# A four-layer Mamba, attention and 13x13 convolution chain on one core: the local gate stays in its PSUM bank, two residual sums move to VectorE, and the last image's and the convolutions' edges are cut finer

## The chip, the cores and the metric

The kernel runs on one core of a Trainium2 chip, as one launch, all in fp32. The metric is the time of one execution on the device in microseconds (us), the median of the executions shown. The engines are TensorE (PE in the profile; its weight load is PEld), VectorE (DVE), ScalarE (ACT) and GpSimd (POOL); SyncE (SP) only issues transfers. SP, ACT and POOL each have a queue of transfers, and the profile shows 16 DMA engines behind them.

## The reference

`x` is (8, 384, 32, 32): B=8 images, C=384 channels, L=1024 pixels. Four layers follow each other:

```
# layer 0, per image, channels last
xn   = rmsnorm(x) * norm_w
u, z = split(xn @ in_proj.T);  u = silu(conv1d(u));  dt, Bm, Cm = split(u @ x_proj.T)
delta = softplus(dt @ dt_proj.T + b)
h[t] = exp(delta*A) * h[t-1] + delta*u*Bm ;  y[t] = sum_n h[t,n]*Cm[n]      # 16 states n
fwd  = ((y + u*D) * silu(z)) @ out_proj.T ;  bwd = the same on the reversed pixels
x1   = x + 0.5 * (0.25*(fwd + bwd) + sigmoid(dwconv3x3(xn) + b) * xn)
# layer 1
h  = conv1x1(bn(x1)); h = dwconv3x3(h); h = conv1x1(bn(h)); x1 = h + x1
q, k, v = conv1x1(x1); out = linear attention with phi(t) = exp(0.5*(2t - t*t)), 8 heads
x2 = x1 + proj(out);  x2 = x2 + mlp(layernorm(x2))                 # 384 -> 1536, gelu, -> 384
# layer 2: a sum of seven depthwise convolutions with bn: one 13x13 kernel per channel
y2 = sum_i bn_i(dwconv_i(x2))
# layer 3
xp = bn(conv1x1(y2)) + y2
out = gelu(bn(dwconv13x13(xp)) + bn(xp*w))
```

The steps that the change touches are the local gate `sigmoid(...)*xn`, the two residual sums `h + x1` and `x1 + proj(out)`, and the ways from one layer to the next after the last image.

## The kernel before

An image has two halves h of 512 pixels and three chunks c (or m) of 128 channels. A product of 128 x 128 weights with 512 columns is issued as four column quarters of 32 (`quarters`, L571, matmul at L575); `dense` (L581) makes three such products, one for each chunk of the input, into one PSUM bank. PSUM has banks under four tags: `mm` (two, `psum`) for short results, `mo` (three, `long_psum`) for results that live longer, `acc` for the scan's sums, and `du`.

**front(b)** (L676) prepares image b: rmsnorm, `project` (in-projection), `branch` (L717, the local gate) and `inner` (conv1d, dt, B and C, written to DRAM for the scan). The gate convolves a half and chunk into a short bank (`conv3`, matmuls at L595 and L600), ScalarE writes tanh from the bank into an SBUF tile `lg` (L725), and two VectorE operations (L728, L731) form `(tanh + 1) * xn` and add it to `xr`, the input read again; a transfer on GpSimd's queue writes the result. These last three are deferred by a step (`defer(1, local)`).

**scan(b)** (L814) goes over 12 units (direction d, half h, chunk c) of four rounds r with two steps i each. A step makes two `da` (exp, ScalarE, L902), `du` (VectorE, L907, into PSUM), two scan instructions `hs` (VectorE, L919), a multiplication by C on GpSimd (L928) and, after both steps, four selector matmuls into `acc` (`sums`, L600). On the way back, the gate `zr` is multiplied in (L875) and `g_d` written (L876, GpSimd's queue).

**layer1(b)** (L1002) reads x1 and g (L1009, L1010), takes the out-projection `op` (L1015, sum on VectorE L1017), the first 1x1 convolution (`h`, L1035), writes it as a padded image to `h_d`, reads that as shifted rows for the 3x3 convolution (`dw`, L638, L1042), then the second 1x1 convolution `c` (L1048), keys and values, `q`, the projection `pj` (L1147), layernorm and the MLP (`mf`, `mo`, L1228 to L1261). The residuals of `c` and `pj` are added by TensorE: an identity product `quarters(ps, ident, o, True, False)` ahead of the three products, and ScalarE evacuates with the bias (L1052, L1151). `last` (L1217) adds the MLP's and writes `x2i_d` on GpSimd's queue; `turn` (L1200) rearranges it into `x2_d`.

**Order of the work.** The driver runs the scans of the eight images in a row (48 rounds each) and, between their rounds, steps of front(b+1) and layer1(b-1) by cost and due time. At `i == rounds - 8` it takes the first step of layer1(b), its loads. A planner at the end of the file (`Plan`, `draft`, the table `BIAS` of rank shifts by engine and kind of instruction) then fixes the order on every engine; names in the profile follow the tiles.

**The tail.** After the last scan come layer1(7), with the loads of the first 20 windows `tp_a` of convolution a's weights on GpSimd's queue between its steps (`windows`), then convolution a (13x13, `conv`, L282 to L384: 96 groups of 32 matmuls over image rows `xt_a`, L364; `put2` writes `y2_d` in fours), the 1x1 convolution `pw` (16 steps t of 3 x 3 products, L410; `yp` read at L419, `xp_d` written at L424) and convolution b. There a GpSimd-queue transfer reads the rows `xt_b` (L323), two VectorE copies shift them (L337), `put3` takes gelu on ScalarE (L432) and writes `out` from GpSimd's queue (L433). Stage edges go through DRAM.

Of the kernel before, what the change touches and what calls it, by code (L numbers as in the profile page):

```python
# [17 lines left out]
P = 128  # L18
C = 384
# [54 lines left out]
def tile_layers(  # L74
# [164 lines left out]
    def load_windows(g_d, tag, n, queues):  # L239

        if not wins:
            wins["pool"] = ctx.enter_context(tc.tile_pool(name="win", bufs=1, side="right"))
        tp = wins["pool"].tile([P, NCH, TP], FP, tag="tp", name=f"tp_{tag}_{n}", bufs=N_WIN)
        for e in range(NSH):
            at = H * ((n % 2 * 2 + e) % NSH)
            win = bass.AP(
                g_d.tensor, g_d[NCH * n, e, 0, 0].offset,
                [[KT, H], [NSH * TG * KT, NCH], [1, TP]],
            )
            queues[e % len(queues)].dma_start(tp[at : at + H], win)  # L250
        wins[tag, n] = tp
# [14 lines left out]
    with tc.tile_pool(name="cx", bufs=2, reuse_waits="tile") as cxp, tc.tile_pool(  # L266
# [15 lines left out]
        def conv(g_d, src_d, last_d, tag, put, far):  # L282
# [13 lines left out]
            def load(n):  # L296
# [10 lines left out]
                if last_d is not None:  # L307
# [12 lines left out]
                src = bass.AP(  # L320
                    src_d.tensor, src_d[NCH * n, 0, 0].offset, [[RL, H], [H * RL, NCH], [1, RL]],
                )
                nc.gpsimd.dma_start(xt[at[0] : at[0] + H], src)  # L323
                xts[n] = xt

            def shift(n):
                at, xt = places(n), xts[n]
                if last_d is not None:
# [45 lines left out]
        def put2(g, ps):  # L374
# [6 lines left out]
            if g % GB == GB - 1:  # L381
                nc.gpsimd.dma_start(y2v[g - GB + 1 : g + 1].rearrange("g p n -> p g n"), hold["t"])
# [20 lines left out]
        for t in range(H // 2):  # L403
            yt = cwp.tile([P, NC, NB], FP, tag="yp", name=f"yp_{t}", bufs=3)
            nc.sync.dma_start(yt, yf[:, :, t * NB : (t + 1) * NB])
            xo = xos[t % 3]
            for m in range(NC):
                ps = cps.tile([P, HALF], FP, tag="cv", name=f"pw_{t}_{m}")
                for k in range(NC):
                    nc.tensor.matmul(  # L410
                        ps[:, 0:NB], pwt[:, k, m * P : (m + 1) * P], yt[:, k, :],
                        start=(k == 0), stop=(k == NC - 1),
                    )
                tm = cwp.tile([P, NB], FP, tag="tm", name=f"tm_{t}_{m}", bufs=3)
                nc.scalar.activation(
                    tm, ps[:, 0:NB], AF.Identity, bias=pbias[:, m, :], scale=bns("pw", m)
                )
                for r in range(2):
                    mid = xo[:, m, r, PADW : PADW + B * (W + PADW)].rearrange("p (b w) -> p b w", w=W + PADW)[:, :, 0:W]  # L419
                    nc.vector.tensor_add(  # L420
                        mid, tm[:, r * BW : (r + 1) * BW].rearrange("p (b w) -> p b w", w=W),
                        yt[:, m, r * BW : (r + 1) * BW].rearrange("p (b w) -> p b w", w=W),
                    )
            nc.gpsimd.dma_start(xf[:, :, 2 * t : 2 * t + 2, :], xo)  # L424
            if t < N_WIN:
                load_windows(g3_d, "b", t, [nc.scalar, nc.sync])
# [3 lines left out]
        def put3(g, ps):  # L430
            ot = cxp.tile([P, BW], FP, tag="ot", name=f"ot_{g}", bufs=6)
            nc.scalar.activation(ot, ps, AF.Gelu, bias=gbias[:, g : g + 1])  # L432
            nc.gpsimd.dma_start(  # L433
# [8 lines left out]
def _layers01(tc, nc, B, xv, x2_d, x2i_d, dram, ident, mean_w, eps5, eps6, one, half, minus1, vec, bns, bnt,  # L442
# [12 lines left out]
    with ExitStack() as ctx:  # L455
# [124 lines left out]
        def dense(ps, w, m, rhs, begin=True):  # L580
            for k in range(NC):  # L581
                product = quarters(
                    ps, w[:, k, m * P : (m + 1) * P], rhs[k] if isinstance(rhs, list) else rhs[:, k, :],
                    begin and k == 0, k == NC - 1,
# [93 lines left out]
        def front(b):  # L678
# [38 lines left out]
            def branch():  # L717
                t3 = tapw(taps3, f"t3_{b}")
                for h in range(2):
                    for c in range(NC):  # L720
# [3 lines left out]
                        lc = t2(f"lg_{b}_{c}_{h}")  # L724
# [9 lines left out]
                        defer(1, local)  # L734
# [77 lines left out]
        newest = []  # L812

        def scan(b):  # L814
# [36 lines left out]
            def sums(k, r, hs, made, acc, y0, zt):  # L851
# [22 lines left out]
                else:  # L874
                    nc.vector.tensor_mul(zt, acc, zt)  # L875
                    nc.gpsimd.dma_start(gv[b][:, c, cols], zt)  # L876
# [125 lines left out]
        def layer1(b):  # L1002


            xx = [None, None]
            w = wtile(outproj_t, f"wo_{b}")
            for h in (1, 0):
                xh, gh = a6(f"xx_{b}_{h}"), a6(f"g_{b}_{h}")
                nc.sync.dma_start(xh, x1v[b][:, :, bass.ts(h, HALF)])  # L1009
                nc.sync.dma_start(gh, gv[b][:, :, bass.ts(h, HALF)])  # L1010
                xx[h] = xh
                yield 0
                for m in range(NC):
                    ps = long_psum(f"op_{b}_{m}_{h}")
                    dense(ps, w, m, gh)  # L1015
                    o = xh[:, m, :]
                    nc.vector.scalar_tensor_tensor(o, ps, rsm, o, ALU.mult, ALU.add)  # L1017
                    yield 3
            w = wtile(c1_d, f"c1_{b}")

            hhs = [image6(f"hh_{b}_{h}") for h in range(2)]
            t3 = tapw(taps3b, f"t3b_{b}")
            dws = [a6(f"dw_{b}_{h}") for h in range(2)]
# [5 lines left out]

            ahead = None  # L1030
            for m, h in ((0, 1), (1, 1), (0, 0), (1, 0), (2, 1), (2, 0)):
                if (m, h) == (2, 0):
                    ahead = ready()
                ps = long_psum(f"h_{b}_{m}_{h}")
                dense(ps, w, m, xx[h])  # L1035
                nc.scalar.activation(hhs[h][1][m], rows(ps), AF.Identity, bias=bias1[:, m, :])
                put_image(h_d, b % 2, h, hhs[h][0], nc.scalar, slice(m, m + 1))
                yield 3
# [7 lines left out]
            for h in range(2):  # L1046
                for m in range(NC):
                    ps = long_psum(f"c2_{b}_{m}_{h}")  # L1048
                    o = xx[h][:, m, :]
                    quarters(ps, ident, o, True, False)  # L1050
                    dense(ps, w, m, dws[h], False)
                    nc.scalar.activation(o, ps, AF.Identity, bias=biasc[:, m, :])  # L1052
# [92 lines left out]
            for h in range(2):  # L1145
                for m in range(NC):
                    ps = long_psum(f"pj_{b}_{h}_{m}")  # L1147
                    o = xx[h][:, m, :]
                    quarters(ps, ident, o, True, False)
                    dense(ps, kvp, m, qps[h], False)  # L1150
                    nc.scalar.activation(o, ps, AF.Identity, bias=vec("proj_b", m))  # L1151
# [46 lines left out]
            behind_gelu = []  # L1198
# [18 lines left out]
            def last(h, acc):  # L1217
                for m in range(NC):
# [4 lines left out]
                    nc.gpsimd.dma_start(x2v[b][:, m, bass.ts(h, HALF)], o)  # L1223
# [4 lines left out]
            for h in range(2):  # L1228
                acc = [long_psum(f"mo_{b}_{h}_{m}") for m in range(NC)]
                for i in range(FF // C):  # L1230
                    wa = wtile(w1_d[:, i * C : (i + 1) * C], f"w1_{b}_{h}_{i}")
                    wb = wtile(w2[i * C : (i + 1) * C, :], f"w2_{b}_{h}_{i}")
                    for fs in [(0, 1), (2,)]:
# [12 lines left out]

                        def second(h=h, i=i, fs=fs, acc=acc, wb=wb, hms=hms):
# [12 lines left out]
            behind_gelu.pop()()  # L1260
# [21 lines left out]
        for b in range(B):  # L1282
            for i, _ in enumerate(scan(b)):
# [4 lines left out]
                if i == rounds - 8:  # L1288
# [483 lines left out]
def draft(nc, tc, bias):  # L1772
# [15 lines left out]
BIAS = {('Activation', 'acc<y0'): -12600,  # L1788
 ('Activation', 'bc_d<xd'): -51300,
 ('Activation', 'center<center'): -83700,  # L1790
 ('Activation', 'da<dlt'): -200,
 ('Activation', 'dl<dt'): -12400,
 ('Activation', 'dw<dw'): -147300,
 ('Activation', 'fold<fold'): -200,
 ('Activation', 'gbias<biasq_d'): -8800,
 ('Activation', 'h_d<hh'): -8500,
 ('Activation', 'hh<h'): -43100,
 ('Activation', 'hm<mf'): -98200,
 ('Activation', 'kp<phi_k'): 21100,
 ('Activation', 'kv<kvs'): 107600,  # L1800
 ('Activation', 'kvp<kvp'): 156300,
 ('Activation', 'lg<lc'): 39500,
 ('Activation', 'ms_r<ms_r'): 1000,
 ('Activation', 'ms_r<ms_s'): -114400,
 ('Activation', 'phi_k<kv_kp'): 98300,
 ('Activation', 'phi_q<q'): -245400,
 ('Activation', 'rz<den'): 1000,
 ('Activation', 'sq<xi'): -34300,
 ('Activation', 'tm<pw'): -16000,
 ('Activation', 'tp_a<g2_d'): -113400,  # L1810
 ('Activation', 'tp_b<g3_d'): 96300,
 ('Activation', 'u_d<uz'): 29000,
 ('Activation', 'uc<c1'): -700,
 ('Activation', 'uz<in'): -7500,
 ('Activation', 'var_r<var_r'): 1500,
 ('Activation', 'var_r<var_s'): -6000,
 ('Activation', 'vs<xx'): -200,
 ('Activation', 'vt<kv_vt'): 2000,
 ('Activation', 'vt<ones'): 5000,
 ('Activation', 'x2_d<turn'): 72600,  # L1820
 ('Activation', 'xd<xd'): -15500,
 ('Activation', 'xx<c2'): 1700,
 ('Activation', 'xx<pj'): -6000,
 ('Activation', 'yf_d<yt'): 5200,
 ('Activation', 'yt<acc'): -96200,
 ('Activation', 'yt<cv_a'): 32000,
 ('Activation', 'z_d<uz'): 28000,
 ('DVE', 'bias1<fold'): -199800,
 ('DVE', 'bias2<bias2'): 108300,
 ('DVE', 'bias2<bn_t'): -1200,  # L1830
 ('DVE', 'bias3<bn_t'): -28500,
 ('DVE', 'biasc<fold'): 59500,
 ('DVE', 'biasf<fold'): -175000,
 ('DVE', 'carry<hs'): 6400,
 ('DVE', 'dlt<pk'): -14500,
 ('DVE', 'du<vr'): -301300,
 ('DVE', 'dwh<pk'): 31000,
 ('DVE', 'g2<kw'): -17200,
 ('DVE', 'g3<k3'): -159500,
 ('DVE', 'hs<da'): 99000,  # L1840
 ('DVE', 'ks<m8'): -28000,
 ('DVE', 'kv<kvs'): 62700,
 ('DVE', 'lg<lg'): -11200,
 ('DVE', 'ln<xx'): -85600,
 ('DVE', 'pbias<pb'): 52300,
 ('DVE', 'pbias<pbias'): 1000,
 ('DVE', 'qp<qp'): -7200,
 ('DVE', 'uc<dl'): -23400,
 ('DVE', 'ud<uc'): -33200,
 ('DVE', 'v2<pk'): 33500,  # L1850
 ('DVE', 'var_r<var_r'): -67300,
 ('DVE', 'var_r<var_s'): -9600,
 ('DVE', 'xn<xi'): 48500,
 ('DVE', 'xo0<tm'): 16000,
# [214 lines left out]
```

## Time and profile before

| | us |
|---|---|
| median of three executions | 4565.47 (4554.04 to 4566.64) |
| the profiled execution | 4564.33 |
| its span / outside the span | 4562.5 / 1.8 |
| busy PE / DVE / POOL / ACT | 4009.3 / 3657.0 / 2771.6 / 2647.7 |
| last scan instruction ends, about | 3614 |
| layer1 of the last image | 3614 to 3972 |
| convolution a | 3982.0 to 4207.9 |
| pw | 4218.1 to 4344 |
| convolution b, last matmul | 4358.3 to 4551.3 |
| mean granted TensorE clock | 0.924 |

The span holds eight scans of about 439 us each (104.9 to 3614, in which an image's 96 steps of du and two scan instructions are about 370 us of VectorE), and the tail of 948 us. A mean busy share says little here: in the scans several engines work side by side, in the tail the stages follow each other. The bracket at the end of a timeline row is the time for which the engine was idle before it and what released it.

### The profile page before, as it was taken

What the parts mean: (1) busy time and instruction counts of PE and PEld (TensorE: products, weight loads), DVE (VectorE), ACT (ScalarE), POOL (GpSimd) and SP (SyncE); (2) the same over time, 40 slices, a digit from 0 to 9 for tenths busy, and PEclk for the clock granted to TensorE, in tenths of its full rate; (3) what the DMA queues carried; (4) which work ended last, traced back from release to release, by engine and by line L of the source; (5) the groups of instructions that cost most, each with busy time, mean ns of one, the idle gap of its engine ahead of it and who ended that gap; (6) DMA issues with size and microseconds to landing.
All of it is one profiled execution on the core that took longest, in us unless ns stands there. A gap on an engine that the chain in (4) does not pass through costs nothing.

```text
span 4562.5 us, 97044 instructions
## 1 busy us (share of the span) xinstructions
PE 4009.3 (88%) x39222; PEld 1573.9 (34%) x39222; DVE 3657.0 (80%) x3749; ACT 2647.7 (58%) x3777; POOL 2771.6 (61%) x1672
## 2 busy tenths in 40 slices
PE   5577699899999999998999999989899789987988
PEld 1122223233433332343223323432232233276467
DVE  2999989999999889998998899899999600175266
ACT  3555657875797578667866786678567413100212
POOL 2677766676667657765776577657676820143079
PEclk8578799999999999999999999999999889998999
DMA  9568776588668866885688668866844761299798
GB/s 259 174 210 273 242 239 209 188 256 264 228 207 254 251 212 204 262 258 198 215 255 249 202 226 261 237 212 215 256 144 162 186 146 48 84 223 229 224 212 183
DMA packets 651130, 975.75 MB, mean 214 GB/s; under 512 B 158280, under 2 KB 333368, under 8 KB 649144
## 3 DMA queue, kind: packets, MB, share of 16 engines
q1 hardware_dynamic: 502064, 676.48, 50.3%
q0 software_dynamic: 53392, 188.07, 13.4%
q10 hardware_dynamic: 95224, 104.98, 7.7%
q8 instruction: 309, 5.06, 0.5%
q14 instruction: 141, 1.16, 0.1%
HBM read 736.63 MB, written 232.67 MB: 212 GB/s over the span
## 4 chain that ended last, share of the span: by engine, by line
PE 42%; issue 15%; DVE 14%; DMA 11%; ACT 6%; POOL 3%; SPq 1%; ACTq 0%; POOLq 0%; DVEq 0%
DVE hs L919 9%; PE mo L575 6%; PE mf L575 6%; DVE du L907 3%; PE pj L575 3%; PE acc L595 3%; PE cv_a L364 2%; PE in L575 2%; PE kv_vt L575 2%; PE c L575 2%; ACT da L902 2%; PE kv_kp L575 2%; DMA tp_a<-g_d 2%; PE q L575 2%; DMA out<-ot 2%
## 5 line engine op out<-in xcount | busy, mean ns | idle before, releaser
L928 POOL TENSOR_TENSOR hs<-hs,bct 128x1024 f32<-128x1024 f32 x768 | 2171.8, 2828 | 845.0 <-DVE carry L924 490.0
L902 ACT ACTIVATE da<-dlt,neg_a 128x512 f32<-128x512 f32 x1536 | 1022.7, 714 | 492.8 <-DVE hs L919 390.6
L907 DVE TENSOR_TENSOR du<-vr,bct 128x1024 f32<-128x1024 f32 x768 | 981.5, 1278 | 49.9 <-DMA vr<-v_d 23.7
L919 DVE TENSOR_TENSOR_SCAN hs<-da,carry,du 128x512 f32<-128x512 f32 x768 | 943.4, 1267 | 37.6 <-ACT da L902 1.0
L919 DVE TENSOR_TENSOR_SCAN hs<-da,du 128x512 f32<-128x512 f32 x768 | 898.3, 1207 | 47.4 <-ACT da L902 15.7
L600 PE MATMUL acc<-hs,selt 128*32 128x512 f32 x2304 | 530.8, 639 | 89.0 <-POOL hs L928 88.9
L575 PE MATMUL mf<-ln,w 128*32 128x512 f32 x4608 | 554.4, 610 | 26.3 <-ACT uc L757 18.6
L575 PE MATMUL mo<-hm,w 128*32 128x512 f32 x4608 | 538.8, 594 | 0.0
L595 PE MATMUL acc<-hs,selt 128*32 128x512 f32 x768 | 416.5, 633 | 41.2 <-POOL hs L928 36.4
L575 PE MATMUL in<-xn,win 128*32 128x512 f32 x2304 | 290.6, 616 | 24.5 <-DMA win<-in_inproj_t 13.9
L902 ACT ACT_TABLE_LOAD x224 | 287.4, 1283 | 40.6 <-DVE hs L919 13.9
L575 PEld LDWEIGHTS mf<-ln,w 128*32 128x32 f32 x4608 | 153.6, 113 | 378.5 <-issue 318.3
L575 PEld LDWEIGHTS mo<-hm,w 128*32 128x32 f32 x4608 | 151.2, 110 | 336.2 <-issue 327.1
L364 PE MATMUL cv_a<-xt_a,tp_a 128*32 128x256 f32 x3072 | 187.2, 398 | 44.8 <-issue 14.7
L1223 POOL DMA_DIRECT2D x2i_d<-xx x48 | 26.6, 555 | 293.8 <-DVE xx L1220 286.3
L364 PE MATMUL cv_b<-xt_b,tp_b 128*32 128x256 f32 x3072 | 180.7, 392 | 26.5 <-DVE xt_b L337 14.2
L600 PE MATMUL dw<-dw_i,t3b 96*32 96x512 f32 x1056 | 192.2, 680 | 10.9 <-DMA dw_i<-h_d 10.7
L337 DVE COPY xt_b<-xt_b 32x2496 f32<-32x2496 f32 x96 | 151.5, 1578 | 50.1 <-DMA xt_b<-xp_d 47.6
L575 PE MATMUL kv_kp<-wk,xx 128*32 128x384 f32 x1536 | 182.2, 487 | 3.9 <-ACT xx L1052 3.7
L364 PEld LDWEIGHTS cv_a<-xt_a,tp_a 128*32 128x32 f32 x3072 | 159.1, 139 | 72.0 <-issue 64.6
L575 PE MATMUL kv_vt<-wv,xx 128*32 128x384 f32 x1536 | 179.7, 491 | 3.8 <-ACT vt L1074 3.8
L600 PEld LDWEIGHTS acc<-hs,selt 128*32 128x32 f32 x2304 | 115.4, 114 | 177.3 <-POOL hs L928 152.3
(211 smaller groups left out, 5855.3 us busy)
## 6 DMA issues: line engine op xcount, KB each, us to landing
dlt<-dl_d SPq DMA_DIRECT2D x384, 256.0 KB, 4.6
vr<-v_d SPq DMA_DIRECT2D x384, 256.0 KB, 5.0
bct<-bc_d SPq DMA_DIRECT2D x256, 256.0 KB, 5.0
ut<-u_d SPq DMA_DIRECT2D x192, 257.5 KB, 5.3
lc_i<-xn_d SPq DMA_DIRECT2D x192, 228.8 KB, 5.9
dw_i<-h_d SPq DMA_DIRECT2D x192, 228.8 KB, 5.8
w<-w_d SPq DMA_DIRECT2D x64, 576.0 KB, 6.3
w<-in_w SPq DMA_DIRECT2D x64, 576.0 KB, 5.0
```

What stands on the lines that cost most here:

```text
L337: nc.vector.tensor_copy(xt[at[e] : at[e] + e * H, :, 0 : RL - e - (e - 1)], xt[at[0] : at[0] + e * H, :, e : RL - (e - 1)],)
L364: nc.tensor.matmul(ps[H * e : H * (e + 1), 0:BW], tp[:, c, :].rearrange("p (j t) -> p j t", t=KT)[:, :, t], rhs, start=(t == 0), stop=(t = ...
L575: product = nc.tensor.matmul(ps[lo:hi], lhs[:, lo:hi], rhs, start=start, stop=stop, skip_group_check=True)
L595: first = product()
L600: tc.keep_in_program_order(product())
L902: nc.scalar.activation(da[:, bass.ts(j, HALF)], dlt[:, bass.ts(j, HALF)], AF.Exp, scale=neg_a[:, g, r : r + 1],)
L907: nc.vector.tensor_mul(pairs(du), pairs(vt), bct[r][:, 0:1, :].to_broadcast([P, 2, HALF]),)
L919: nc.vector.tensor_tensor_scan(t[:, s][:, way], da[:, s][:, way], du[:, s][:, way], k_c if second else 0.0, ALU.mult, ALU.add,)
L928: made.append(nc.gpsimd.tensor_mul(pairs(t), pairs(t), bct[r][:, 1:2, :].to_broadcast([P, 2, HALF])))
L1223: nc.gpsimd.dma_start(x2v[b][:, m, bass.ts(h, HALF)], o)
```

## The change

1. **The gate.** tanh is written into the PSUM bank that holds the convolution (`lc = ps`), and the two VectorE operations read it there; they are issued at once, not deferred.
2. **Residuals.** `c` and `pj` lose the identity product; VectorE adds product, bias and residual in one operation in place of ScalarE's evacuation.
3. **The last image's right half (h=1)** goes on into its first 1x1 convolution inside the scan: its weights are loaded in the scan and the driver takes a step of layer1(7) in each of the last rounds. The last unit's gated output stays in SBUF (`newest_g`), and the left half's g is read chunk by chunk. Only the left half's convolution remains after the scans.
4. **The end of the last image's MLP.** For its last steps, the second products are kept and done chunk by chunk, with the sum and the write of each chunk behind it; the writes go on SP's queue.
5. **Convolution edges.** The last four groups of a are written one by one; pw's first two steps read their input and multiply chunk by chunk; its last three steps go chunk by chunk over the output, each written at once; the windows of b are loaded behind the start of pw's products; the first rows of b are read as four shifted transfers on SP's and ScalarE's queues; `out` is written from ScalarE's queue.
6. **The table `BIAS`** has some 180 new values, and the whole order is planned anew.

In the built programs TensorE has 19227 matmul instructions in place of 19611 (384 fewer), VectorE 3845 in place of 3751, ScalarE 2756 activations in place of 2852 and 565 table loads in place of 545; transfers issued by GpSimd go from 690 to 585, by ScalarE from 555 to 653, by SP from 2379 to 2402.

```diff
-                        lc = t2(f"lg_{b}_{c}_{h}")
+                        lc = ps
                         nc.scalar.activation(lc, ps, AF.Tanh, bias=dwh[:, c, :], scale=0.5)
...
-                        defer(1, local)
+                        local()
...
                 else:
                     nc.vector.tensor_mul(zt, acc, zt)
-                    nc.gpsimd.dma_start(gv[b][:, c, cols], zt)
+                    if b == B - 1 and k == len(units) - 1:
+                        newest_g.append(zt)
+                    else:
+                        nc.gpsimd.dma_start(gv[b][:, c, cols], zt)
...
+                if final and h == 0:
+                    rhs = [gh[:, 0, :], gh[:, 1, :], newest_g[0]]
+                    for k in range(NC - 1):
+                        nc.sync.dma_start(gh[:, k, :], gv[b][:, k, bass.ts(h, HALF)])
...
+                if final and h == 1:
+                    w1c = wtile(c1_d, f"c1_{b}")
+                    hhs[h] = image6(f"hh_{b}_{h}")
+                    for m in range(NC):
+                        first(m, h)
+                        yield 3
...
-            for m, h in ((0, 1), (1, 1), (0, 0), (1, 0), (2, 1), (2, 0)):
+            for m, h in ((0, 0), (1, 0), (2, 0)) if final else ((0, 1), (1, 1), (0, 0), (1, 0), (2, 1), (2, 0)):
...
                     ps = long_psum(f"c2_{b}_{m}_{h}")
+                    dense(ps, w, m, dws[h])
                     o = xx[h][:, m, :]
-                    quarters(ps, ident, o, True, False)
-                    dense(ps, w, m, dws[h], False)
-                    nc.scalar.activation(o, ps, AF.Identity, bias=biasc[:, m, :])
+                    nc.vector.scalar_tensor_tensor(o, ps, biasc[:, m, :], o, ALU.add, ALU.add)
...
                     ps = long_psum(f"pj_{b}_{h}_{m}")
+                    dense(ps, kvp, m, qps[h])
                     o = xx[h][:, m, :]
-                    quarters(ps, ident, o, True, False)
-                    dense(ps, kvp, m, qps[h], False)
-                    nc.scalar.activation(o, ps, AF.Identity, bias=vec("proj_b", m))
+                    nc.vector.scalar_tensor_tensor(o, ps, vec("proj_b", m), o, ALU.add, ALU.add)
...
+                        if b == B - 1 and h == 1 and i >= FF // C - 2:
+                            rest += [(i, f, hm, wb) for f, hm in zip(fs, hms)]
+                            yield 7
+                            continue
...
+            for m in range(NC):
+                for i, f, hm, wb in rest:
+                    quarters(
+                        acc[m], wb[:, f, m * P : (m + 1) * P], hm, False, i == FF // C - 1 and f == NC - 1,
+                    )
+                if rest:
+                    last(1, acc, [m])
...
-                if i == rounds - 8:
+                if i == rounds - 8 or (b == B - 1 and i > rounds - 7):
                     next(seconds[b])
...
-            if g % GB == GB - 1:
+            if g >= NQ - GB:
+                nc.sync.dma_start(y2v[g], hold["t"][:, g % GB, :])
+            elif g % GB == GB - 1:
...
+        for k in range(NC):
+            for t in range(2):
+                for m in range(NC):
+                    product(t, m, [k])
...
+        for m in range(NC):
+            for t in range(NT - 3, NT):
+                product(t, m, range(NC))
+                finish(t, m)
+                queue = nc.gpsimd if m == 0 else nc.sync
+                queue.dma_start(xf[:, m, 2 * t : 2 * t + 2, :], xos[t % 3][:, m, :, :])
...
+                for e in range(NSH if n == 0 else 1):
+                    src = bass.AP(
+                        src_d.tensor, src_d[NCH * n, 0, e].offset, [[RL, H], [H * RL, NCH], [1, RL - e]],
+                    )
+                    queue = [nc.sync, nc.scalar][e % 2] if n == 0 else nc.gpsimd
+                    queue.dma_start(xt[at[e] : at[e] + H, :, 0 : RL - e], src)
...
             nc.scalar.activation(ot, ps, AF.Gelu, bias=gbias[:, g : g + 1])
-            nc.gpsimd.dma_start(
+            nc.scalar.dma_start(
```

## The prediction

> **What bounds the kernel now.** I first read the page's busy shares and 40 slices (114 us each; PEclk is the granted TensorE clock in tenths), then tables by windows, groups by line and form, and TensorE's timeline of the tail.
>
> ```profile
> PE 4009.3 (88%) x39222; PEld 1573.9 (34%) x39222; DVE 3657.0 (80%) x3749; ACT 2647.7 (58%) x3777; POOL 2771.6 (61%) x1672
> PE   5577699899999999998999999989899789987988
> DVE  2999989999999889998998899899999600175266
> DMA  9568776588668866885688668866844761299798
> ```
>
> Until slice 31 VectorE is at 8 or 9 tenths with TensorE beside it; from slice 32 (3650 us) VectorE is nearly idle. The scans end at 3614 us and the span at 4562.5: 948 us of tail, four stages in a row, where TensorE's gaps are time.
>
> The table by windows inside the scans (columns: window, length, busy PE, PEld, DVE, ACT, POOL, clock, DMA share, GB/s):
>
> ```profile
> 700.00:1100.00 400.00, 362.36 (x3483) 120.25 (x3479) 382.64 (x387) 299.85 (x407) 275.28 (x144) 0.95 0.71 227
> 1100.00:1200.00 100.00, 98.85 (x1186) 46.53 (x1182) 86.86 (x71) 54.37 (x98) 65.75 (x25) 0.99 0.78 234
> 2900.00:3000.00 100.00, 99.51 (x1220) 44.87 (x1212) 79.66 (x69) 57.36 (x102) 62.91 (x25) 1.00 0.76 230
> 700.00:3600.00 2900.00, 2693.13 (x26187) 942.95 (x26183) 2690.59 (x2670) 2087.87 (x2912) 1964.04 (x969) 0.96 0.71 223
> ```
>
> Two engines share the bound, both at 2690 of 2900 us: VectorE leads for most of an image (383 of 400), TensorE in its attention part (98.9 and 99.5 of 100, VectorE 80 to 87).
>
> The groups by line and form (busy us, mean ns | idle before, releaser):
>
> ```profile
> L728 DVE SCALAR_TENSOR_TENSOR lg<-lg,one,xn 128x512 f32<-128x512 f32 x48 | 85.1, 1772 | 37.6 <-ACT lg L725 37.4
> L731 DVE SCALAR_TENSOR_TENSOR xr<-lg,rsh,xr 128x512 f32<-128x512 f32 x48 | 49.5, 1033 | 26.1 <-DMA xr<-in_x 17.5 <-issue 7.2 <-DMA dlt<-dl_d 0.3
> L1017 DVE SCALAR_TENSOR_TENSOR xx<-op,rsm,xx 128x512 f32<-128x512 f32 x48 | 35.5, 742 | 38.9 <-PE op L575 38.6
> L1151 ACT ACTIVATE xx<-pj,pk 128x512 f32<-128x512 f32 x48 | 32.9, 685 | 65.2 <-PE pj L575 65.0
> L433 POOL DMA_DIRECT2D out<-ot x96 | 138.4, 1446 | 15.3 <-DVE xt_b L337 7.6 <-ACT ot L432 7.5
> ```
>
> The same VectorE operation at the same size takes 1772 and 1033 ns with both tensors in SBUF, and 742 with one in PSUM (L1017): that row prices the changed ones. The tail, by TensorE's timeline (start, length, in brackets the idle time before and its releaser):
>
> ```profile
> 3645.19 9.80 PE L575 MATMUL op<-g,wo 128*32 128x512 f32 x72 [24.05 <-DMA g<-g_d]
> 3674.51 1.89 PE L595 MATMUL dw<-dw_i,t3b 96*32 96x512 f32 x2 [4.06 <-issue]
> 3982.04 9.63 PE L364 MATMUL cv_a<-xt_a,tp_a 128*32 128x256 f32 x128 [10.02 <-POOL xt_a L313]
> 4218.13 125.99 PE L410 MATMUL pw<-yp,pwt 128*128 128x512 f32 x288 [10.27 <-DMA yp<-y_d]
> 4358.32 6.95 PE L364 MATMUL cv_b<-xt_b,tp_b 128*32 128x256 f32 x86 [14.20 <-DVE xt_b L337]
> ```
>
> Four stage edges, 58.5 us idle. After the second line the 3x3 convolutions take 47 us (3674.5 to 3721.3) for six at about 3.9: their loads share the DMA engines with the first convolution's 80 windows (DMA share 1.02 and 1.05 of 3650 to 3700).
>
> **The change part by part.** Our measurement tells 0.3% (14 us) from no change.
>
> *Gate in the bank.* 48 times two VectorE operations go from 1772 and 1033 to 742: per image 6 × (1030 + 291) ns = 7.9 us less. The bank was free after tanh (683 ns); now it waits for both operations, in order behind a du (1.28) and two scans (1.27 and 1.21), at most 3.8 us before each. Queued behind them is any later product needing one of two short banks, and behind that, on TensorE, the scan's sums. Cost: nothing if another bank is free, 48 × 4 = 192 if each hold stalls TensorE. The trace has six gates in 72 us (1134 to 1206), 12 apart, so I take zero; if that cover goes, see the slower rival.
>
> *Residuals.* Twelve identity products per image go (one product of four quarters: 0.87 us, op x72 being nine in 9.80, h x144 18 in 15.64): 10.4 us of TensorE. Twelve ScalarE evacuations of 0.685 go, twelve VectorE operations of 0.742 come: +8.9. In the scan VectorE's account is therefore −7.9 + 8.9 = +1.0 us per image, TensorE's −10.4, ScalarE's −8.2; the order has 20 more table loads (545 to 565) of 1.283, 25.7 us, on ScalarE, 72% busy there: zero. Seven images have this part inside scans. If VectorE decides all, 7 us are lost; if TensorE does, 73 won. Its own stages are where TensorE leads, but VectorE catches the gain after about a third: 3.4 × 7 = 24. By the rows each evacuation becomes 57 ns dearer on VectorE (0.742 against 0.685), 0.7 us per image. The Trainium skill, "VectorE: DVE Perf Modes", Specifications, puts VectorE closer to SBUF and ScalarE closer to PSUM, which speaks against moving an evacuation from PSUM to VectorE; it gives no size there, and the term by it would be somewhat under the 24.
>
> *Last image.* The right half's first products and c1 run before the last scan's end, and the last unit's gate output stays in SBUF. In the new order only two thirds of the left half's op remain beside the scan and its last third after it. The 24.05 stall goes, and with it half of h (7.8 of 15.64): 31.8. Next late are the 3x3 loads (L638, now earlier but still against the windows); where they took 47, they give back 0 to 17. I take 25 (15 to 35). Its own identity products, where nothing else runs: 12 × 0.87 = 10.4, minus 57 ns each: 9 (5 to 10). These products pass acc and hs in the last rounds: at most 6 × 2.6 us on TensorE, which had 0.75 to 0.97 load there: zero, bounded by 15 lost within the range.
>
> *MLP's end by channel group*: of the 10.02 edge a last write, a read and a first shift remain: 7 (3 to 10). *Convolution a to pw*: 5.49 idle before its last 40 records plus 10.27; last groups written singly, first products by chunk: 8 (4 to 14). *pw to b*: 14.20; the shift L337 (1.6 us) goes, reading by four DMAs replaces it, a write of one chunk remains: 11 (7 to 14). *Convolution a* takes 226 us (3982.0 to 4207.9) where 96 groups of 1.83 (the timeline has 128 records, four groups, in 7.35) are 176, at a DMA share of 1.04 (4020 to 4192). The window loads for b, which began at 4131.8, now wait for the first pw products, a third of the stage becomes freer, and single writes and first chunks are added: 4 (−5 to 15). Those windows then land within pw's 126 us, at a share of 0.71: zero.
>
> *Output on ScalarE's queue.* Per step GpSimd issues two out (1.446 mean, up to 2.1) and one xt_b (1.098); b takes 193 us where 176 would do. GpSimd is 88% to 100% busy:
>
> ```profile
> 4400.00:4450.00 50.00, 43.60 (x727) 35.51 (x721) 36.03 (x25) 10.26 (x24) 44.12 (x34) 0.93 1.10 245
> 4450.00:4500.00 50.00, 47.31 (x841) 40.61 (x834) 37.44 (x24) 10.87 (x25) 48.31 (x37) 1.00 1.03 235
> 4500.00:4530.00 30.00, 28.31 (x490) 23.95 (x485) 24.22 (x16) 7.55 (x16) 30.00 (x22) 1.00 0.77 166
> ```
>
> ScalarE (21% busy) can issue: gain 0 to 17, and 2 to 6 of the 11.2 between the last product and the end. But the DMA share is over 1 until 4500, so only after it is issuing clearly the limit: 8 + 4. "Trainium Kernel Development and Optimization", Key Constraints, says that DMAs issued from these queues all run on the same 16 engines and several queues save only issue time; by that rule the first 100 us of b give nothing and the term would be about 4 + 4.
>
> The sum: 25 + 9 + 7 + 4 + 8 + 11 + 8 + 4 = 76 in the tail, 24 in the scans, 100 together. The profiled execution is 4564.3 (span 4562.5 and 1.8 outside), the median of three 4565.5: 4564.3 − 100 is 4464, with the median's 1.1 4465. The whole order is planned again (the table of shifts is replaced); its effect has no row, between a loss of 30 and a gain of 30 (VectorE's idle 7% of an image, 30 us of 439, halved in one or repeated in two of the seven), taken at zero.
>
> **The rivals.** *Given back*: the tail's transfers decide. Lower ends: 15 + 5 + 3 − 5 + 4 + 7 + 0 + 2 = 31, and in the scans VectorE loses 7: 24, so 4541; with half of them, around 4520. For it: DMA shares over 1 in three places of the tail. Against: 24.05 is one wait in a queue behind other loads, with TensorE at 6 of 30 us.
>
> *TensorE was the bound*: the scans give up to 73 and re-planning some, the tail the same 76 or its upper 100: 4564 − 73 − 100 = 4391; typical 4415. For it: 99.5 of 100 in the attention windows. Against: 383 of 400 for VectorE elsewhere.
>
> *The bank is held (slower)*: place, the six gates of each image; one of two short banks stays taken until the second VectorE operation, and TensorE, in order, stops with sums and attention products behind it. Price p for each gate, 48 times. From p = 100/48 = 2.1 us it eats the whole gain; with one VectorE turn (3.8) it is 48 × 3.8 = 182 − 100 = 82 slower: 4647. For it: TensorE has no slack where the gates lie (1134 to 1206). Against: 12 us between gates, and three banks more for the long products.
>
> *VectorE alone decides and the order changes nothing*: 76 − 7 = 69, 4496, within my range.
>
> **How the numbers follow.** Forecast (4430 to 4500, with the case of VectorE alone) 0.51, time 4465; TensorE was the bound (4390 to 4430) 0.17; given back (4500 to 4551) 0.19; no change 0.03; slower 0.10, of which most is the bank. The range 4395 to 4540 leaves out the slower case, no change, and some of the two ends. Faster 0.51 + 0.17 + 0.19 = 0.87.
>
> **What would show it.** Right: L728 and L731 at 0.72 to 0.76 us; no ident products at c and pj; scans ending 15 to 35 us earlier than 3614; no 24 us gap before dw; edges of 2 to 5 us; convolution b near 183 to 190. Wrong: TensorE waiting on lg or xr before a short bank (the held bank); scans ending no earlier with VectorE over 94% busy (VectorE alone); the dw stage at 47 us or longer and b at 193 with DMA share over 1 (given back). The prediction fails if the scans alone move by over 60 us either way.

## The result and the profile after

The changed kernel takes 4487.78 us (4480.11 to 4490.59), before 4559.76 over the same comparison: a ratio of 0.984, 95% interval 0.9816 to 0.9864, 72 us less. The forecast was 4465, in the range 4395 to 4540. The total lies within the range, 23 us above the forecast; several of its terms did not hold. This table takes each stage from the timelines of the two profiled executions (spans 4562.5 and 4487.8), in us:

| stage | before | after | gain | predicted |
|---|---|---|---|---|
| scans, first du to the last scan's end | 3510.0 | 3467.9 | 42.1 | 24 |
| to the end of the 3x3 convolutions | 107.4 | 95.3 | 12.1 | 25 |
| from there to convolution a | 259.8 | 246.0 | 13.8 | 9 + 7 |
| a's first matmul to pw's first | 236.1 | 196.0 | 40.1 | 4 + 8 |
| pw's first to b's first | 140.2 | 140.9 | −0.7 | 11 |
| b's first matmul to the end | 204.2 | 237.1 | −32.9 | 8 + 4 |

The page after:

```profile
PE 3960.7 (88%) x38454; PEld 1600.2 (36%) x38454; DVE 3643.9 (81%) x3843; ACT 2618.5 (58%) x3701; POOL 2615.8 (58%) x1567
DMA  9587786588658866896788668856845661398998
```

The groups by line and form: the two gate operations, and the two new residual sums.

```profile
L776 DVE SCALAR_TENSOR_TENSOR lc<-lc,one,xn 128x512 f32<-128x512 f32 x48 | 35.9, 748 | 1.8 <-ACT lc L773 1.7
L779 DVE SCALAR_TENSOR_TENSOR xr<-lc,rsh,xr 128x512 f32<-128x512 f32 x48 | 35.9, 748 | 11.2 <-DMA xr<-in_x 10.3
L1217 DVE SCALAR_TENSOR_TENSOR xx<-pj,pk,xx 128x512 f32<-128x512 f32 x48 | 35.7, 744 | 23.6 <-PE pj L623 23.4
L1119 DVE SCALAR_TENSOR_TENSOR xx<-c,biasc,xx 128x512 f32<-128x512 f32 x48 | 35.7, 744 | 142.6 <-PE c L623 142.5
```

All four cost what L1017 foretold (742 ns). TensorE's timeline at the edges of the tail (start, length, idle before and releaser):

```profile
3603.65 1.88 PE L643 MATMUL dw<-dw_i,t3b 96*32 96x512 f32 x2 [15.93 <-DMA dw_i<-h_d]
3913.78 16.27 PE L371 MATMUL cv_a<-xt_a,tp_a 128*32 128x256 f32 x256 [10.86 <-DVE xt_a L338]
4109.78 3.68 PE L427 MATMUL pw<-yp,pwt 128*128 128x512 f32 x8
4222.49 21.15 PE L427 MATMUL pw<-yp,pwt 128*128 128x512 f32 x42 [3.37 <-DMA yp<-y_d]
4250.67 16.96 PE L371 MATMUL cv_b<-xt_b,tp_b 128*32 128x256 f32 x256 [7.03 <-issue]
4310.09 9.07 PE L371 MATMUL cv_b<-xt_b,tp_b 128*32 128x256 f32 x128 [4.26 <-ACT ot L480]
```

The 24 us gap on g is gone, but another of 15.93 on the 3x3 rows stands in its place. The edge to a is as wide as before (10.86 for 10.02), the one to pw closed (10.27 before), the one to b halved (14.20 before), and inside b TensorE now waits for ScalarE's gelu, `ot`.

### The profile page after: what moved, and what is told of

Same layout as the page of the kernel before. It is cut to its first block, busy times and chain, and to the rows that moved or that the text cites. A ratio compares the mean times of both kernels' runs of the same rounds, so it can differ in the third digit from the quotient of the medians.

```text
span 4487.8 us, 95449 instructions
## 1 busy us (share of the span) xinstructions
PE 3960.7 (88%) x38454; PEld 1600.2 (36%) x38454; DVE 3643.9 (81%) x3843; ACT 2618.5 (58%) x3701; POOL 2615.8 (58%) x1567
## 2 busy tenths in 40 slices
DMA packets 748530, 976.06 MB, mean 217 GB/s; under 512 B 256840, under 2 KB 433464, under 8 KB 746552
## 4 chain that ended last, share of the span: by engine, by line
PE 49%; DVE 18%; DMA 15%; issue 7%; ACT 6%; POOL 2%; SPq 1%; ACTq 1%; DVEq 0%; POOLq 0%
DVE hs L970 11%; PE mo L623 8%; PE mf L623 7%; DVE du L958 4%; DMA dw_i<-h_d 3%; PE cv_a L371 3%; PE acc L643 3%; PE pj L623 3%; PE cv_b L371 2%; ACT da L953 2%; PE in L623 2%; PE q L623 2%; PE op L623 2%; PE kv_vt L623 2%; PE c L623 2%
## 5 line engine op out<-in xcount | busy, mean ns | idle before, releaser
L623 PE MATMUL mf<-ln,w 128*32 128x512 f32 x4608 | 579.1, 614 | 36.6 <-ACT uc L805 20.4
L623 PE MATMUL mo<-hm,w 128*32 128x512 f32 x4608 | 564.1, 595 | 0.3 <-DVE xx L1286 0.3
L623 PE MATMUL in<-xn,win 128*32 128x512 f32 x2304 | 307.6, 629 | 24.7 <-DMA win<-in_inproj_t 15.4
L623 PEld LDWEIGHTS mf<-ln,w 128*32 128x32 f32 x4608 | 167.1, 113 | 383.9 <-issue 299.2
L623 PEld LDWEIGHTS mo<-hm,w 128*32 128x32 f32 x4608 | 166.9, 110 | 325.3 <-issue 293.9
L648 PE MATMUL dw<-dw_i,t3b 96*32 96x512 f32 x1056 | 222.0, 686 | 16.2 <-DMA dw_i<-h_d 16.1
L371 PE MATMUL cv_b<-xt_b,tp_b 128*32 128x256 f32 x3072 | 192.6, 410 | 47.3 <-ACT ot L480 37.9
L313 POOL DMA_DIRECT2D xt_a<-x_d x48 | 40.1, 835 | 303.8 <-PE var_b L623 121.4
L344 DVE COPY xt_b<-xt_b 32x2496 f32<-32x2496 f32 x94 | 136.4, 1452 | 88.0 <-DMA xt_b<-xp_d 78.9
L371 PEld LDWEIGHTS cv_b<-xt_b,tp_b 128*32 128x32 f32 x3072 | 147.3, 143 | 92.9 <-ACT ot L480 45.3
L623 PEld LDWEIGHTS in<-xn,win 128*32 128x32 f32 x2304 | 99.8, 115 | 196.4 <-issue 156.4
## 6 DMA issues: line engine op xcount, KB each, us to landing
lc_i<-xn_d SPq DMA_DIRECT2D x192, 228.8 KB, 6.5
dw_i<-h_d SPq DMA_DIRECT2D x192, 228.8 KB, 6.2
```

The lines of the kernel that those rows point to most:

```text
L313: nc.gpsimd.dma_start(own[:, 0:near], src_d[n].rearrange("h b c w -> h (b c w)"))
L344: nc.vector.tensor_copy(xt[at[e] : at[e] + e * H, :, 0 : RL - e - (e - 1)], xt[at[0] : at[0] + e * H, :, e : RL - (e - 1)],)
L371: nc.tensor.matmul(ps[H * e : H * (e + 1), 0:BW], tp[:, c, :].rearrange("p (j t) -> p j t", t=KT)[:, :, t], rhs, start=(t == 0), stop=(t = ...
L623: product = nc.tensor.matmul(ps[lo:hi], lhs[:, lo:hi], rhs, start=start, stop=stop, skip_group_check=True)
L648: tc.keep_in_program_order(product())
```

## Experiments: why convolution b became longer

All twelve kernels are compared with the kernel before on the same chip; stages are read from each one's profile as in the table above. One execution of each is profiled: the kernel before and the same kernel with only `out` moved (below), in the same order on TensorE and VectorE, differ by 2.5 us in the scans and by 6 in the stage from a to pw, where `out` plays no part, so a few us in a stage are scatter.

**Output back on GpSimd's queue** (changed kernel). With the queue, these issues get back the rank that they had in the planner's table before:

```diff
-            nc.scalar.dma_start(
+            nc.gpsimd.dma_start(
...
- ('Activation', 'out<ot'): 4700,
+ ('Pool', 'out<ot'): -67300,
```

> The changed kernel with only the output's transfers of convolution b back on GpSimd's queue; the planned order of TensorE and VectorE is the same as in the changed kernel. Convolution b with the end took 237 us there (4250.7 to 4487.8) and 204 before. Theory P (packets: from ScalarE's queue each output transfer becomes 1024 packets of 128 bytes, some 98,000 more packets under 512 B, and the 16 DMA engines, already full, need longer) and theory S (ScalarE's gelu stands behind the issues of out and of the windows in one queue) both expect about 204 again, total 4450 to 4460. Theory O (out is innocent; the later windows or the first rows of b cost it) expects 230 to 237, total 4480 to 4490.

Measured: 4466.47, ratio 0.9796 (0.9778 to 0.9814); b with its end 207.7. Theory O falls: the queue of `out`, with the place of its issues, is worth 29 us of that stage. The total is 6 us above the range of P and S.

**Output on SP's queue** (`nc.sync`, rank 4700 as in the changed kernel).

> The changed kernel with the output's transfers on SP's queue, where no computing engine stands behind them. Theory P expects the packets as many and as small as on ScalarE's queue and convolution b with its end at 225 to 240, total 4475 to 4490. Theory S expects about 200, total 4445 to 4455.

Measured: 4472.86, 0.9808 (0.9787 to 0.9829); b with its end 218.9. Between both theories: 11 us above GpSimd's queue, 18 below ScalarE's.

**The kernel before with `out` on ScalarE's queue** (rank -67300, as in the kernel before).

> The kernel before with only the output's transfers moved to ScalarE's queue; the order of TensorE and VectorE is that of before. Theories P and S: convolution b with its end from 204 to 230 to 240 us, total 4585 to 4600. Theory O: 195 to 206, total 4550 to 4562.

Measured: 4566.44, 1.0017 (1.0005 to 1.0029); b with its end 216.1, 12 more than before. The direction is P's and S's, the size less than half of what I expected of them: on ScalarE's queue the cost was 12 here, with rank -67300, and 33 in the changed kernel, with 4700. TensorE's waits differ too: here 25.1 us for the window loads `tp_b` and 6.0 for `ot`.

**ScalarE's queue, another rank** (changed kernel, in the planner's table; `out` stays on ScalarE):

```diff
- ('Activation', 'out<ot'): 4700,
+ ('Activation', 'out<ot'): -67300,
```

> The changed kernel with out still on ScalarE's queue, but planned there with the rank that it had on GpSimd's (-67300 in place of 4700): only ScalarE's order changes. Convolution b with its end: 237 us with the changed kernel's order, 219 with out on SP's queue, 208 on GpSimd's. Theory S2 (what ScalarE's queue cost above SP's is the place of window and output issues ahead of the gelu): 214 to 224, total 4465 to 4477. Theory S1 (any issuing on ScalarE costs it, whatever the place): 230 to 240, total 4480 to 4492.

Measured: 4468.56, 0.98 (0.9772 to 0.9828); b with its end 212.8, 1 us below S2's range and far from S1's. S2 holds: 24 of the 29 us were the places of the issues in ScalarE's order. The rank is not all of that order: the changed kernel with the old table (below) has -67300 too, and its b takes 224.8. The changed kernel's timeline shows the mechanism; ACTq are issues that ScalarE makes itself, and its gelu stands behind them:

```profile
4301.33 5.16 ACTq L250 DMA_DIRECT2D tp_b<-g_d  x2
4306.59 2.93 ACTq L481 DMA_DIRECT2D out<-ot  x2
4309.56 0.47 ACT L480 ACTIVATE ot<-cv_b,gbias 128x256 f32<-128x256 f32 x1 [7.77 <-DMA out<-ot]
```

TensorE's row of 4310.09 above, released by this gelu, had waited 4.26. The group of b's matmuls in the stage, first in the changed kernel, then with `out` on GpSimd's queue, on SP's, and on ScalarE's with the other rank (busy, mean ns | idle and releasers):

```profile
L371 PE MATMUL cv_b<-xt_b,tp_b 128*32 128x256 f32 x3072 | 192.6, 410 | 47.3 <-ACT ot L480 37.9 <-issue 9.3
```
```profile
L371 PE MATMUL cv_b<-xt_b,tp_b 128*32 128x256 f32 x3072 | 180.6, 392 | 25.4 <-ACT ot L480 9.6 <-DMA xt_b<-xp_d 7.9 <-DVE xt_b L344 4.6
```
```profile
L371 PE MATMUL cv_b<-xt_b,tp_b 128*32 128x256 f32 x3072 | 185.6, 401 | 36.3 <-DMA tp_b<-g_d 26.4 <-DMA xt_b<-xp_d 7.7 <-issue 2.1
```
```profile
L371 PE MATMUL cv_b<-xt_b,tp_b 128*32 128x256 f32 x3072 | 184.3, 396 | 32.1 <-ACT ot L480 21.4 <-DMA xt_b<-xp_d 7.8 <-issue 2.7
```

On ScalarE the waits are for `ot` (37.9), on SP for window loads (26.4). SP issues half of these windows, and there `out` stands ahead of them and waits for the gelu (total us, times, longest):

```profile
SPq L481 <- ACT ot L480: 55.4, 46, 4.6
```

So SP's 11 us are in part, perhaps all, an order of issues as well; SP's queue with the other rank was not run. What packets can explain is the 5 us that are left with the other rank on ScalarE's queue (212.8 for 207.7). GpSimd's queue (software) and ScalarE's (q10) in the changed kernel, then with `out` back on GpSimd (packets, MB, share of 16 engines):

```profile
q0 software_dynamic: 47616, 170.88, 11.7%
q10 hardware_dynamic: 195608, 118.21, 9.9%
```
```profile
q0 software_dynamic: 52224, 183.47, 13.1%
q10 hardware_dynamic: 95768, 105.62, 8.0%
```

The same 12.6 MB of output are 99,840 packets on ScalarE's queue, 1040 for each transfer, and 4,608 on GpSimd's, 48 for each. On SP's they are 99,840 again. The stage by windows, with ScalarE's queue and the other rank, then with GpSimd's (the last three figures are the clock, the DMA share and GB/s):

```profile
4256.80:4469.00 212.20, 184.26 (x3072) 149.47 (x3072) 133.87 (x94) 45.16 (x96) 44.73 (x44) 0.97 1.06 201
```
```profile
4254.00:4461.00 207.00, 180.64 (x3072) 153.55 (x3072) 145.76 (x94) 43.76 (x96) 180.11 (x140) 0.96 0.96 206
```

Both move 42.6 MB, but share times length is 225 us of busy DMA engines (mean of the 16) with the small packets and 199 without. That is theory P's direction; its 5 us of the stage are no more than the scatter, and no run varies the packets alone.

**Last eight groups only** (GpSimd's queue for 88, ScalarE's for the last 8):

> The changed kernel with out on GpSimd's queue for the first 88 groups of convolution b and on ScalarE's for the last 8. P and S: as with all on GpSimd's queue, and the end after the last matmul 4 to 6 us in place of 11, total 4443 to 4455. O: 4478 to 4488.

Measured: 4461.76, 0.9781 (0.9753 to 0.9808); b with its end 204.0. The end after the last matmul is 8.4, not 4 to 6, and the total 7 above its range.

## Experiments: what the scans gained from

**Gate alone** on the kernel before (`lc = ps`, `local()`).

> The kernel before with the gate in the PSUM bank alone (two VectorE operations read the bank, not deferred), planned anew with the old table. The scans went from 104.9 to 3614.9 before, 3510 us. Theory V (VectorE decides the scans): 7.9 us per image less on VectorE, 45 to 60 less in the scans, total 4495 to 4515. Theory T (TensorE decides): 0 to 15 less, total 4545 to 4560. Theory H (the held bank stops TensorE): over 40 more, total above 4600. Theory N (a new order by itself is worth tens of us either way) expects any of these and is read from the third kernel.

Measured: 4540.70, 0.9966 (0.9952 to 0.9981); scans 3495.2, 14.8 less. The stage is T's, the total lies between T and V. H falls.

**Residual sums alone** on the kernel before.

> The kernel before with the two residual sums on VectorE alone. Theory V: 8.9 us per image more on VectorE, the scans 30 to 60 us longer, the last image's part 9 shorter, total 4580 to 4615. Theory T: 10.4 us per image less on TensorE, the scans 40 to 70 shorter and the last image's part 9, total 4480 to 4510. In between (my forecast): 15 to 30 shorter in all.

Measured: 4559.57, 1.0004 (0.9992 to 1.0016); scans 3533.3, 23.3 more; the way from the 3x3 convolutions to convolution a 12.8 less. The scans go V's way, by less than V's 30 to 60, and the total did not move where I had forecast 15 to 30 less. The next run shows that a new order of unchanged work can cost 29 us in the scans, so the sign of these 23 is not shown to be the sums' own.

**Table alone** on the kernel before.

> The kernel before with the changed kernel's table of rank shifts and nothing else: the same work in another order. Theory N: the total moves by 15 us or more. Theories V and T (the work decides) expect within 15 us of before, 4545 to 4572.

Measured: 4573.86, 1.0034 (1.002 to 1.0047); scans 3538.8, 28.8 more. N: with the same work an order can cost that much.

**Gate, residual sums and table** on the kernel before.

> The kernel before with gate, residual sums and the changed table, without the last image's early start and without the convolutions' edges. Alone, the gate took 15 us off the scans, the residual sums added 23, the table added 29. Theory F (the table was fitted to these two): scans 3455 to 3475, as in the changed kernel. Theory A (the parts add): near 3510 + 37 = 3547, and the changed kernel's scans owe their time to the last image's part or to chance in the order.

Measured: 4503.83, 0.9869 (0.9855 to 0.9884); scans 3470.8, as F says. **The changed kernel with the old table**:

> The changed kernel with the table of rank shifts of before (the renamed kinds take the old entries). The scans took 3510 us with the old work and the old table, 3539 with the old work and the new table, 3468 with the new work and the new table. Theory N (table and work count together, a table fits the work it was fitted to): 3500 to 3530. Theory V/T (the new work alone gains): 3460 to 3485.

Measured: 4506.61, 0.9874 (0.9857 to 0.989); scans 3456.3. So F is wrong in its reason: with the new work the old table scans as fast or faster. What the kernels with short scans share is the two parts together: 39 to 54 us less, where their single effects add up to 8.5 more. (The kernel with 54 also has the other parts of the change.) That is more than chance in the order shows: two other plans of the old work lie 4 below it (the windows' kernel below) and 29 above. The medians with the two tables lie 19 us apart (4506.6 and 4487.8); in the profiled executions the tail is 13 us shorter with the new table and the scans 12 longer. The table by windows, each kernel over its scans, in the order before, gate, residuals, both with the table, changed (the third figure after the length is VectorE's busy time):

```profile
104.90:3614.90 3510.00, 3146.45 (x29433) 1080.05 (x29434) 3262.16 (x3237) 2439.96 (x3418) 2385.87 (x1191) 0.93 0.71 224
```
```profile
104.90:3600.10 3495.20, 3138.40 (x29375) 1061.74 (x29378) 3223.69 (x3234) 2482.66 (x3450) 2382.58 (x1189) 0.94 0.71 225
```
```profile
107.30:3640.60 3533.30, 3109.52 (x28753) 1078.79 (x28756) 3343.36 (x3320) 2428.81 (x3361) 2388.39 (x1191) 0.93 0.70 223
```
```profile
112.40:3583.20 3470.80, 3105.95 (x28804) 1100.97 (x28806) 3257.15 (x3323) 2417.48 (x3356) 2386.89 (x1191) 0.93 0.73 228
```
```profile
104.60:3572.50 3467.90, 3110.61 (x28918) 1116.61 (x28922) 3255.52 (x3323) 2418.76 (x3357) 2387.49 (x1193) 0.94 0.73 228
```

Read each as VectorE busy plus VectorE idle. Gate: 38 less busy, 24 more idle (248 to 272). The two gate rows fell by 63, as priced, but other rows of VectorE grew, `du` by 14 (1278 to 1296 ns, 768 times). Residuals: 81 more busy, 58 less idle. Of the 96 sums, 84 lie in the scans, 62 of these 81 us, and the first of the unchanged gate rows grew from 1772 to 2173 ns, 19 us. Both: busy as before (−5), idle 214, 34 less. I read it so: TensorE's saving turns into time where VectorE has room, and the gate makes that room.

## Experiments: the tail

**Windows of b held behind pw**, alone on the kernel before.

> The kernel before with only the windows of convolution b held behind pw's first products. Convolution a from its first matmul to pw's first took 236 us before and 196 in the changed kernel. Theory W (those window loads, issued from ScalarE's queue ahead of its evacuations, held convolution a up): 205 to 215. Theory E (the single writes and first reads by chunk did it): 230 to 240. The scans are planned anew, so the stage is to be compared and not the total.

Measured: 4541.35, 0.9964 (0.9951 to 0.9977); the stage 217.6, 3 us outside W's range and far from E's. But the gate's, the residuals' and the table's kernels, with neither, are at 226.7, 222.0 and 220.9, and the order of before gave 230.1 in another execution: that order, and the execution profiled, were poor ones here, and most of the 18.5 us cannot be given to the windows.

**Windows of a late**: the kernel with the last eight `out` on ScalarE, and the first of the 80 loads made to wait for the fourth 3x3 convolution's evacuation (`MARK` keeps the two instructions' names).

```diff
...
+        held = mybir.DependencyInfo(mybir.DependencyClass.Sync, mybir.DependencyReason.DATA)
+        tc.add_manual_dep(by[MARK["window", "a"]], MARK["dw", B - 1, 1], held, reason="windows late")
```

> The kernel with out on ScalarE's queue for the last 8 groups only, and in it the first of the 80 window loads of convolution a made to wait for the evacuation of the fourth 3x3 convolution of the last image; the order on every engine is unchanged. From the last scan's end to the end of the 3x3 convolutions it took 95.8 us, with a DMA share of 1.02 to 1.04 from 3580 to 3660 and under 0.35 after it until convolution a. Theory D (those loads hold up the 3x3 convolutions' rows): 55 to 65 us, the total 30 to 40 less, 4420 to 4435. Theory L (the chain write h, read rows, convolve sets it whatever else moves): 90 to 96, the total unchanged at 4455 to 4470, or later if the windows come too late for convolution a.

Measured: 4420.89 (4415.57 to 4422.56), 0.9686 (0.967 to 0.9702); from the last scan to the end of the 3x3 convolutions 52.7 in place of 95.8. Theory D, and a little more: the fastest version here, 41 us below the same kernel without the wait (4461.76) and 67 below the changed one. The windows of the changed kernel (two), then of this one, and the issue lines of the 3x3 rows (KB each, median us to landing) in the same two:

```profile
3600.00:3620.00 20.00, 13.34 (x30) 1.82 (x30) 0.00 (x0) 0.59 (x1) 10.92 (x19) 0.57 1.04 213
3660.00:3680.00 20.00, 20.00 (x172) 11.39 (x172) 2.25 (x3) 1.17 (x2) 0.00 (x0) 0.87 0.27 64
```
```profile
3600.00:3620.00 20.00, 19.03 (x90) 3.95 (x93) 0.00 (x0) 1.76 (x3) 0.00 (x0) 0.84 0.88 227
```
```profile
dw_i<-h_d SPq DMA_DIRECT2D x24, 228.8 KB, 16.4
```
```profile
dw_i<-h_d SPq DMA_DIRECT2D x24, 228.8 KB, 6.2
```

In the changed kernel 80 window loads that nobody needs for some 300 us fill the engines (1.04) while the 3x3 rows are read, and the share falls to 0.27 when they are done. TensorE's waits for these rows add up to 30.4 us in the stage there and 7.4 here. Starting the convolutions earlier only moved them fully under that load.

## Why the prediction was right, and where its steps were not

**Right in the total by terms that offset each other.** From the table, the scans (42 for 24) and the way from a to pw (40 for 12) gave 46 more than forecast; the 3x3 part, the edges after the MLP and after pw, and b gave 72 less (13, 2, 12, 45). The forecast of the sum, 100, came out at 75 in the profiled pair. Two signs that I had set for the rival "given back" came true, the 3x3 part longer than 47 us and b longer than 193, so part of that rival is in the result. The scans ended 41 us before 3614, outside the 15 to 35 that I had named. That such misses cancel to within 25 us is luck, and so is part of the scans and of convolution a: I took the new order at zero, and a new order of unchanged work made the scans 29 longer and the way from a to pw 15 shorter.

**Right: the gate and residual prices.** 748 and 744 ns. VectorE's busy time in the scans moved by −7 us, forecast +7. The Trainium skill's "VectorE: DVE Perf Modes", Specifications, has VectorE closer to SBUF and ScalarE closer to PSUM. The sums cost 744 against 685 on ScalarE, which goes that way, but they are not the same operation; and on VectorE itself the gate was slower with both tensors in SBUF (1772 and 1033) than with one in PSUM (748), so that here the measured rows decide and not the place.

**Right mechanism, size off: TensorE's saving.** I let a third of the 73 us through. VectorE's idle time fell by 35 (248 to 212), half of it. What I had not seen is that the parts need each other: with the residual sums alone the scans were no shorter (23 longer, within what a new order can cost).

**Fallen rival: the held bank.** It exists and is small. In the changed kernel's waits from 110 to 3572 five rows have TensorE released by `xr` L779, 12.5 us together, 0.26 for each gate; the point where it decides was 2.1.

**Half right: the 3x3 part.** The stall went and half of `h` with it: the first row came 28.5 us earlier after the last scan (31.1 for 59.6). The convolutions then took 64 us in place of 48. I had the collision in the sum and let it give back 0 to 17, so 25 remained; it gave back 16, the end of the range that I did not take. The last kernel shows the cause.

**Wrong: the MLP's end** by chunk, 7 forecast. The edge stayed (10.86), though its first part shrank: VectorE's first copy of the image rows began 7.0 us after the last product in the kernel before, 3.3 in the changed one. The step that failed is "a first shift": that copy took 1.42 us before and 5.99 after, where GpSimd's memsets of `xo` run beside it. The copy before, then copy and memsets after:

```profile
3979.06 1.42 DVE L331 COPY xt_a<-xt_a 32x2440 f32<-32x2440 f32 x1 [6.21 <-DMA xt_a<-x_d]
```
```profile
3906.06 4.88 POOL L279 MEMSET xo<- 128x1878 f32 x3 [16.41 <-DMA x2i_d<-xx]
3906.23 5.99 DVE L338 COPY xt_a<-xt_a 32x2440 f32<-32x2440 f32 x1 [2.48 <-DMA xt_a<-x2i_d]
```

In the changed kernel with the old table the memsets come later, the copy takes 1.42 and the edge is 7.17. Of the 13.8 us of that stage 12.8 came with the residual sums alone, where 9 were forecast for the identity products; a new order alone gave 5.4.

**Wrong: pw to b**, 11 forecast. The edge gave 7.2, and pw's own products with their waits took as much more: 133.9 us to the edge in place of 126.0, with waits on `yp` and a DMA share of 1.00 from 4110 to 4250 in place of 0.69. Windows loaded in this stage are not enough for that: with them alone the stage stayed at 140.1 with a share of 0.96. That leaves the orders by chunk at its two ends and the new planned order; no run separates them.

**Wrong, and the largest: output on ScalarE's queue**, 12 forecast, −33 measured. The step that failed is "ScalarE (21% busy) can issue": busy time says nothing of an engine whose next instruction stands behind an issue that waits. I priced GpSimd's issues and not what queues behind ScalarE's. Of the 33 us, 24 are the place of the issues in ScalarE's order, 5 what is left between the two queues, and 4 remain with `out` on GpSimd's. The shorter end did come, 4.2 after the last matmul for 11.2. The rule of the Trainium skill that I weighed, "Trainium Kernel Development and Optimization", Key Constraints, that all queues share the 16 engines, pointed to less than my term, and by my estimate still to a gain. The skill's "DMA: Bandwidth & Descriptors", Specifications, wants 512 B or more for line rate; here packets under 512 B went from 158,280 to 256,840, and in b's stage the 16 engines were busy for 225 us with them and 199 without; no run here shows what the size of the pieces alone does.

**Open: convolution a.** Of its 40 us, 10 are the edge to pw (a's last matmul and pw's first lay 10.3 apart, now 0.6), and 6 are scatter of the execution before (230.1 in the other). The kernels above with another order, and no new edges, are 9 to 15 below 236.1; the one with the windows alone is 18.5 below. Edges with the old table reach 205.3, with the new one 196.0; with the old table, though, pw begins ahead of a's last products, which end 213.8 us after its first (195.4 with the new table). Which edit gave what of the remainder is not settled.

## What to carry to other kernels

Before moving a transfer to another engine's queue, list what stands behind the issue on that engine and when it waits, and count the packets that the queue makes of it; an engine's busy share answers neither. An edge that is started earlier ends earlier only if the transfers that it needs find the DMA engines free: look for loads in that window that are needed much later, since holding these back was worth as much (43 us in that stage) as the largest gain of the change. Where two engines share a bound, price edits together: here the gate alone gave 15 us in the scans, the residual sums alone none, and the two together 39 to 54. And ask what another engine does beside a short step on the critical path: a copy on the edge to convolution a lost 4.6 us beside memsets.

## What the runs showed that I had not expected

- One 128 KB output transfer in pieces of 128 bytes is 1040 packets on ScalarE's or SP's queue and 48 on GpSimd's.
- The 3x3 rows' transfers of 228.8 KB land in a median of 6.2 us with the window loads held back and 16.7 in the same kernel without that wait (16.4 in the changed one).
- One VectorE copy of 32x2440 took 5.99 us with three GpSimd memsets beside it, and 1.42 without.
- The same work in another planned order took 0.34% longer as a whole (0.2 to 0.47), while one stage, convolution a to pw, was 15 us shorter.
